# Parts of the projection's matrix on SyncE's queue behind a reading, with rooms of later buffers for odd groups

## The chip, the cores and the metric

The kernel runs on one core of a Trainium2 chip. The metric is device time in microseconds of one execution, as the median of several runs. The engines are TensorE (PE, matmuls; PEld is its weight load), VectorE (DVE), ScalarE (ACT), GpSimd (POOL) and SyncE (SP), which only starts transfers here. A letter q behind an engine's name in the profile (SPq, ACTq) is its instruction queue, with the DMAs that it issues.

## The reference

Two layers over x of 8 sequences x 512 rows x 256 columns, both with a norm before and after and a residual sum: grouped attention, then a mixture of experts. The change touches the last product of the attention (`out @ wo`).

```python
def _L0_attn_ref(x, wq, bq, wkv, bkv, wo):
    G, QPG, D = (4, 4, 128)
    b, t, e = x.shape
    q = (x @ wq + bq).reshape(b, t, G, QPG, D).transpose(0, 2, 3, 1, 4)
    kv = (x @ wkv + bkv).reshape(b, t, G, 1, 2 * D).transpose(0, 2, 3, 1, 4)
    k, v = (kv[..., :D], kv[..., D:])
    pe = sinusoidal_pe(t, D, x.dtype)
    q = q + pe
    k = k + pe
    scores = jnp.einsum('bgqtd,bgksd->bgqts', q, k) / math.sqrt(D)
    scores = jnp.where(causal, scores, -jnp.inf)
    probs = jax.nn.softmax(scores, axis=-1)
    out = jnp.einsum('bgqts,bgksd->btgqd', probs, v).reshape(b, t, G * QPG * D)
    return out @ wo
...
x = x + _layernorm(_L0_attn_ref(_layernorm(x), ...))
x = x + _layernorm(_L0_ffn_ref(_layernorm(x), ...))
```

`_L0_ffn_ref` routes each of the 4096 rows to 6 of 64 experts (at most 64 rows per expert and sequence block) and adds a shared expert. All numbers are float32.

## The kernel before, in words

**Steps.** The attention is a loop over k from 0 to 127: 8 sequences b, in each 4 groups of heads g, in each 4 steps. 16 steps are a sequence; a step handles one quarter of a group's score blocks for 4 heads at once. I number groups through: n = 4 b + g, so group n has the steps 4n to 4n + 3. The order of the instructions on every engine is written out by hand in this loop (`manual_schedule`), and each engine's queue is worked off in that order.

**One step's chain.** `scores(k, q)` (L518 to L526) makes four blocks of scores on TensorE (psc); VectorE adds the mask and takes the smallest (L522), ACT takes the exponential in place (e, L526). `weigh(k)` divides by the sum on GpSimd (L536). In the next step `turned(k)` (L550) turns the weights in 32 x 32 blocks on VectorE into eb (L554), writes eb to DRAM in four DMAs of 160 KB on SyncE's queue (ex_d, L558), waits there for their landing, and reads them back in the other order as et in one DMA of 640 KB (L564). In the step after that `mix(k)` multiplies et with the values on TensorE (pav, L591), and ACT moves the result into ao (L602). So a step's writes and reading stand in step k + 1, and its pav near the end of step k + 2. Two such buffers exist (ex_d[0], ex_d[1]; et with two tiles).

**Other users of SyncE's queue.** Behind the reading come the reading of the next sequence's x, an exchange of normalised rows through DRAM (exr_d; `xr` and `xt`, the latter feeding the shared expert's product psg, L1094), stores of xg, y and the output. ACT's queue carries the store of x1 (L1170), and from step 94 on the experts' weights (wgu, wd: 32 times 352 KB three times over).

**The projection.** For sequences 0 and 7 a step pair's ao is multiplied with a whole group's part of wo (`project`, L616), of which `load_whole` (L204) loads one group at a time (512 KB, tile tag "wc", one buffer). For sequences 1 to 6 (`CROSSED`) it is done by a scheme with seven products instead of eight on sums and differences of blocks: `make_sets` (L625) stores for each of the four groups two sets of blocks in DRAM during sequence 0, ws_d (3 blocks, 384 KB) and wc_d (4 blocks, 512 KB). `straight(j)` (the products ps) uses a ws set, `across(j)` (pc) a wc set, both through `multiply` (L666). `load_set` (L642) loads a group's set, ws into a tile with tag "ws", wc into one with tag "wc", one buffer each. The products of group n stand in steps 4n + 4 to 4n + 7: ps in 4n + 4 and 4n + 6, pc in 4n + 5 and 4n + 7 (for the last group of a sequence both pc stand in even steps or right behind ps).

**When the sets are loaded.** `load_sets(k)` (L1382) is called in step k behind `weigh(k)` and issues on ACT's queue: ws of group n in step 4n + 3, wc of group n in step 4n + 4, that is one step ahead of the products that use them. The whole parts are issued on ACT's queue at the end of steps 6, 10, 14, 114, 118, 122 and 126.

**Semaphores of transfers.** In the built program the DMAs of SyncE and ACT take eight semaphores (DMAHW0 to DMAHW7) in turn. A DMA that takes a semaphore whose last DMA came from the other queue, or is not yet known to have landed, first waits for that landing. So a write of ex_d can wait for a load that ACT issued: in the program before, the fourth write of step 26's weights waits for ws of group 6.

**Buffers that the change borrows.** p3's tag "gx" (three buffers, rows gathered for a pair of experts, L897), p3's "dd" (three buffers, a pair's results, L962) and p2's "gt" (one buffer, L830 and later). The experts' work that uses them begins in step 94.

Of the kernel before, what the change touches and what calls it, by code (L numbers as in the profile page):

```python
# [11 lines left out]
F32 = mybir.dt.float32  # L12
# [7 lines left out]
P = 128  # L20
B, T, E = 8, 512, 256
NT = B * T
NI = T // P
# [4 lines left out]
G, QPG, D = 4, 4, 128  # L28
NH = G * QPG
# [10 lines left out]
EARLY = 5  # L40
# [4 lines left out]
CROSSED = range(1, B - 1)  # L45

@with_exitstack
def sandwich_kernel(ctx, tc, x, wq, bq_t, wkv, bk_t, bv, wo, gate_wt, w_gate, w_up, w_down,
                    sh_gate_t, sh_up_t, sh_down_t, pe_t, out):
    nc = tc.nc  # L50
# [20 lines left out]
    ws_d = [dram.tile([P, 3, 2, P], F32, tag=f"ws{g}_d", name=f"ws{g}_d") for g in range(G)]  # L71
    wc_d = [dram.tile([P, 4, 2, P], F32, tag=f"wc{g}_d", name=f"wc{g}_d") for g in range(G)]
# [83 lines left out]
    with ExitStack() as part:  # L156
        def pool(name, bufs):
            return part.enter_context(tc.tile_pool(name=name, bufs=bufs))

        wpool = pool("weights", 1)  # L160
        p1 = pool("p1", 1)
        p2 = pool("p2", 2)
        p3 = pool("p3", 2)
# [40 lines left out]
        def load_whole(n):  # L204

            t = whole[n] = wpool.tile([D, QPG, E], F32, tag="wc", name=f"wo_{n}")
            nc.scalar.dma_start(out=t, in_=wo.rearrange("(h d) e -> d h e", d=D)[:, ts(n % G, QPG), :])

        load_whole(0)
        partial = wpool.tile([P, 2, 7, P], F32, tag="partial", name="partial")  # L210

        sg_sb, su_sb = [wpool.tile([P, NC, FSH + NX // 2], F32, tag=name, name=name) for name in ("sg_sb", "su_sb")]
        for half, (t, w) in enumerate(((sg_sb, sh_gate_t), (su_sb, sh_up_t))):
            nc.sync.dma_start(out=t[:, :, :FSH], in_=w.rearrange("(c p) n -> p c n", p=P))
            nc.sync.dma_start(out=t[:, :, FSH:],
                              in_=gate_wt.rearrange("(c p) n -> p c n", p=P)[:, :, ts(half, NX // 2)])
# [65 lines left out]
        po = {}  # L282
# [246 lines left out]
        def weigh(k):  # L529
            l = live[k]  # L530
            recip = small.tile([P, NI], F32, tag="recip", name=f"recip_{k}")
            nc.vector.reciprocal(recip, l["total"])  # L532
            engine = nc.gpsimd if k < NK - 1 else nc.vector
            for q in range(NI):
                e = blocks_of(k, q)
                engine.tensor_scalar(e, e, recip[:, q : q + 1], 1.0, ALU.mult, ALU.mult)  # L536
# [82 lines left out]
        crossed, outs, sets = {}, {}, {}  # L619
# [5 lines left out]
        def make_sets(g):  # L625

            w = blocks_of_whole(whole[g])
            t = p1.tile([P, 4, 2, P], F32, tag="xt2", name=f"sets_{g}")
            for k in range(2):
                nc.scalar.dma_start(out=ws_d[g][:, k], in_=w[:, k, 0])  # L630
            nc.scalar.dma_start(out=wc_d[g][:, 0], in_=w[:, 1, 1])
            nc.gpsimd.tensor_sub(t[:, 0], w[:, 0, 1], w[:, 0, 0])
            nc.gpsimd.tensor_sub(t[:, 1], w[:, 1, 1], t[:, 0])
            yield
            nc.gpsimd.tensor_sub(t[:, 2], w[:, 1, 1], w[:, 0, 1])
            nc.gpsimd.tensor_sub(t[:, 3], w[:, 1, 0], t[:, 1])
            yield
            nc.scalar.dma_start(out=wc_d[g][:, 1:], in_=t[:, :3])
            nc.scalar.dma_start(out=ws_d[g][:, 2], in_=t[:, 3])
            yield  # L640

        def load_set(n, d, name):  # L642
            t = wpool.tile(list(d[0].shape), F32, tag=name, name=f"{name}_{n}")
            nc.scalar.dma_start(out=t.rearrange("p k n e -> p (k n e)"), in_=d[n % G].rearrange("p k n e -> p (k n e)"))
            sets.setdefault(n, {})[name] = t

        def sides_of_results(j):

            (x11, x12), (x21, x22) = [[results[j][:, u].rearrange("d (n k) q -> d k n q", k=2)[:, k] for k in range(2)]
                                      for u in range(2)]  # L650
            return x11, x12, x21, x22
# [10 lines left out]
        def multiply(j, factors, name, tag):  # L662
            bank_ = ps_o.tile([P, len(factors[0]), P], F32, tag=tag, name=f"{name}_{j}")
            for pair in range(2):
                for n, (a, w) in enumerate(factors[pair]):
                    nc.tensor.matmul(bank_[:, n, :], lhsT=a, rhs=w, start=pair == 0 and n == 0,  # L666
                                     stop=pair == 1 and n == len(factors[0]) - 1, skip_group_check=True)
            return bank_

        def straight(j):  # L670
            x11, x12, _, x22 = sides_of_results(j)
            w = sets[j // 2]["ws"]
            po[j, 0] = multiply(j, [[(x[:, n], w[:, k, n]) for k, x in enumerate((x11, x12, x22))] for n in range(2)],
                                "ps", "o0")

        def across(j):
            w, t = sets[j // 2]["wc"], crossed.pop(j)
            po[j, 1] = multiply(j, [[(t[:, k, n], w[:, k, n]) for k in range(4)] for n in range(2)], "pc", "o1")

        def add_up(j, part):  # L680
            b, n = divmod(j, 2 * G)
# [26 lines left out]
        def projections(k):  # L708

            j, odd, b, n, last = projected(k)  # L710
            if j < 0:
                return
            if b not in CROSSED:
                for i in () if odd else tiles_at(j):
                    project(j, i)
            elif not odd:
                straight(j)
            elif not last:
                across(j)
# [6 lines left out]
        def projections_behind(k):  # L726
            j, odd, b, n, last = projected(k)
            if b in CROSSED:
                if not odd:
                    add_up(j, 0)  # L730
                elif not last:
                    add_up(j, 1)
                if last and not odd:
                    across(j)
# [644 lines left out]
        values(0, 0, 1)  # L1379
        behind, ahead, making = {}, iter(()), iter(())  # L1380

        def load_sets(k):  # L1382

            n, step = divmod(k, NI)
            if step == 3 and (n // G) in CROSSED:
                load_set(n, ws_d, "ws")
            if step == 0 and n and (n - 1) // G in CROSSED:
                load_set(n - 1, wc_d, "wc")

        routed, zeroing = experts(), zeros()  # L1390
        twice, finishing = False, 0
# [5 lines left out]
        for k in range(NK):  # L1397
# [28 lines left out]
            if k < 2:  # L1426
                queries(k + 2)
            weigh(k)
            load_sets(k)
            if b <= EARLY and s == 7:  # L1430
                next(ahead)()
            side(s, "A")
# [54 lines left out]
            if k % NI == 0 and 1 <= k // NI <= G:  # L1487
                making = make_sets(k // NI - 1)
            next(making, None)
            if k % NI == 2 and k // NI and k // NH not in CROSSED:  # L1490
                load_whole(k // NI)
            side(s, "D")
# [26 lines left out]
        with tc.For_i(0, table["rest"], 1) as n:  # L1519
# [5 lines left out]
            for b in range(EARLY, B):  # L1525
                q, tag = [(p1, "hid"), (wpool, "e0"), (wpool, "e1")][b - EARLY]
                xg = q.tile([P, NI, LROW], F32, tag=tag, name=f"rest_xg_{b}")
                nc.sync.dma_start(out=xg, in_=rows_of(lxg_d, b * T - ET_ROWS))
                q, tag = [(p1, "y"), (p2, "x"), (p1, "xt2")][b - EARLY]
# [73 lines left out]
```

## Time and profile before

| | us |
|---|---|
| three runs | 1398.02, 1405.69, 1407.23 |
| median | 1405.69 |
| profiled execution | 1402.7 |
| its span, first to last instruction | 1400.9 |
| mean granted clock of TensorE | 0.99 |

The profile covers one execution. It lists for each engine the time in which it was busy, for each idle stretch what ended it (the releaser), and for each DMA queue the packets. Queue 1 is SyncE's, queue 10 ACT's:

```profile
## 3 DMA queue, kind: packets, MB, share of 16 engines
q1 hardware_dynamic: 127053, 204.67, 50.2%
q10 hardware_dynamic: 47568, 73.67, 16.3%
q0 software_dynamic: 6144, 9.44, 3.3%
```

The transfers that the following speaks of, with their number and size:

```profile
ex_d<-eb SPq DMA_DIRECT2D x504, 160.0 KB
et<-ex_d SPq DMA_DIRECT2D x126, 640.0 KB
wc<-wc_d ACTq DMA_DIRECT2D x24, 512.0 KB
```

ws is loaded 24 times with 384 KB, whole parts of wo 8 times with 512 KB, all on ACT's queue. In a row of the timeline the first number is the start in us from the span's start, the second the duration, xN the number of instructions merged; the bracket tells how long the engine was idle before it and what ended that. A DMA's row in a queue is its issue, not its transfer.

### The profile page before, as it was taken

The page shows a single profiled execution, that of the slowest core. Times are in us where ns is not written, and L with a number is a line of the kernel's source. Part 1 is how long each engine was busy: PE and PEld are TensorE (multiplying, and loading weights), DVE is VectorE, ACT ScalarE, POOL GpSimd, SP SyncE. Part 2 cuts the span into 40 slices and gives each one's busy share as a digit, 9 for nine tenths or more (in the row PEclk, how much of TensorE's full clock was granted, in tenths as well). Part 3 has the DMA queues.
Part 4 walks back from the last instruction along what each step waited for, and adds up shares of the span by engine and source line. Part 5 has one row for each costly group of instructions (what it writes and reads, how often), then busy time and mean ns, then how long its engine had stood idle before and what let it go on. Part 6 is the DMA issues. An engine that isn't in the chain of part 4 may idle for free. (4 is left out here: it accounts for less than half of the span.)

```text
span 1400.9 us, 22036 instructions
## 1 busy us (share of the span) xinstructions
PE 1333.5 (95%) x6842; PEld 1024.3 (73%) x6842; DVE 917.1 (65%) x2943; ACT 548.4 (39%) x1667; POOL 641.2 (46%) x1052
## 2 busy tenths in 40 slices
PE   9999989999999999999999999998999999989897
PEld 6887776787777776787778776786767677767674
DVE  5575567866777677776787678776557545666544
ACT  3333344334433353334443353333443334434523
POOL 4444243336433553436442553346555554755611
PEclk9999999999999999999999999999999999999999
DMA  6677777655674667655765566679999989877712
GB/s 217 184 235 223 202 222 213 191 163 177 199 206 135 195 189 216 192 160 172 234 184 161 174 206 189 175 214 271 294 312 265 272 237 316 207 240 234 253 59 69
DMA packets 180883, 289.20 MB, mean 206 GB/s; under 512 B 18956, under 2 KB 148461, under 8 KB 180765
## 3 DMA queue, kind: packets, MB, share of 16 engines
q1 hardware_dynamic: 127053, 204.67, 50.2%
q10 hardware_dynamic: 47568, 73.67, 16.3%
q0 software_dynamic: 6144, 9.44, 3.3%
q8 instruction: 55, 0.90, 0.3%
q14 instruction: 63, 0.52, 0.1%
HBM read 172.11 MB, written 115.61 MB: 205 GB/s over the span
## 5 line engine op out<-in xcount | busy, mean ns | idle before, releaser
L536 POOL TENSOR_SCALAR e<-e,recip 128x512 f32<-128x512 f32 (+1 forms) x504 | 245.2, 523 | 507.6 <-DVE recip L532 436.2
L526 ACT ACTIVATE e<-e,least 128x32 f32<-128x32 f32 (+1 forms) x504 | 258.4, 514 | 263.9 <-DVE least L522 243.5
L591 PE MATMUL pav<-et,v 128*128 128x256 f32 x1280 | 307.9, 389 | 41.6 <-DMA et<-ex_d 39.9
L591 PEld LDWEIGHTS pav<-et,v 128*128 128x128 f32 x1280 | 243.6, 194 | 89.9 <-DMA et<-ex_d 23.8
L518 PE MATMUL psc<-kt,qt 128*128 128x32 f32 (+15 forms) x1024 | 276.6, 408 | 3.6 <-DVE least L522 2.2
L522 DVE CUSTOM_DVE_ANT_0 e<-psc,mask 128x32 f32<-128x32 f32 (+1 forms) x504 | 203.9, 430 | 109.0 <-PE psc L518 106.6
L602 ACT ACTIVATE ao<-pav,bv_sb 128x256 f32<-128x256 f32 x255 | 107.2, 471 | 399.8 <-PE pav L591 366.7
L518 PEld LDWEIGHTS psc<-kt,qt 128*128 128x128 f32 x1024 | 161.0, 191 | 64.9 <-DVE least L522 29.1
L554 DVE STREAM_TRANSPOSE eb<-e 128x1024 f32<-128x1024 f32 (+1 forms) x252 | 197.5, 822 | 2.1 <-POOL e L536 1.5
L666 PEld LDWEIGHTS pc<-wc,crossed 128*128 128x128 f32 x768 | 92.5, 192 | 7.8 <-issue 4.3
L666 PE MATMUL pc<-wc,crossed 128*128 128x128 f32 x768 | 94.5, 276 | 0.8 <-POOL crossed L660 0.8
L526 ACT ACTIVATION_READ_ACCUMULATOR e<-e,least 128x1 f32 x504 | 94.4, 187 | 0.0
L666 PEld LDWEIGHTS ps<-ws,ao 128*128 128x128 f32 x576 | 71.6, 192 | 18.2 <-issue 8.4
L971 POOL DMA_INDIRECT y_d<-dd,idx x32 | 50.8, 1588 | 66.7 <-DMA y_d<-dd,idx 22.1
L378 PE MATMUL pq<-xnt,wq_sb 128*128 128x256 f32 x320 | 75.6, 380 | 0.0
L331 DVE SCALAR_TENSOR_TENSOR kt<-pk,bk_sb,pe_sb 128x512 f32<-128x512 f32 x32 | 24.0, 749 | 74.7 <-PE pk L329 72.4
L666 PE MATMUL ps<-ws,ao 128*128 128x128 f32 x576 | 72.3, 275 | 0.3 <-DMA ws<-ws_d 0.3
L422 PE MATMUL pq_back<-rows_joined,heads 128*128 128x256 f32 x264 | 71.3, 379 | 0.0
L340 PEld LDWEIGHTS pv<-wkv_sb,xnt 128*128 128x128 f32 x512 | 65.9, 192 | 4.5 <-issue 1.1
L340 PE MATMUL pv<-wkv_sb,xnt 128*128 128x128 f32 x512 | 67.5, 275 | 0.5 <-ACT ao L602 0.5
L378 PEld LDWEIGHTS pq<-xnt,wq_sb 128*128 128x128 f32 x320 | 59.1, 190 | 10.8 <-issue 1.9
L422 PEld LDWEIGHTS pq_back<-rows_joined,heads 128*128 128x128 f32 x264 | 50.2, 190 | 16.2 <-issue 8.2
(259 smaller groups left out, 1951.9 us busy)
## 6 DMA issues: line engine op xcount, KB each, us to landing
ex_d<-eb SPq DMA_DIRECT2D x504, 160.0 KB
et<-ex_d SPq DMA_DIRECT2D x126, 640.0 KB
wc<-wc_d ACTq DMA_DIRECT2D x24, 512.0 KB
wgu<-in_w_gate ACTq DMA_DIRECT2D x32, 352.0 KB
wgu<-in_w_up ACTq DMA_DIRECT2D x32, 352.0 KB
wd<-in_w_down ACTq DMA_DIRECT2D x32, 352.0 KB
ws<-ws_d ACTq DMA_DIRECT2D x24, 384.0 KB
y<-y_d ACTq DMA_DIRECT2D x10, 512.0 KB
```

Source lines behind the costliest of these rows:

```text
L340: nc.tensor.matmul(pv[:, i, :], lhsT=s["xnt"][:, c, ts(2 * n + i, P)], rhs=wkv_sb[:, c, g, 1, :], start=c == 0, stop=c == NC - 1, skip_gro ...
L378: nc.tensor.matmul(pq[:, n, :, :], lhsT=wq_sb[g][:, c, ts(2 * pair + n, D)], rhs=seqs[b]["xnt"][:, c, :].rearrange("p (u v) -> p u v", v=P ...
L422: nc.tensor.matmul(out, lhsT=factor[0], rhs=factor[1], start=first, stop=last, skip_group_check=True)
L518: nc.tensor.matmul(psc[:, :w], lhsT=halves[k // 2][:, at, :, :].rearrange("d h t -> d (h t)"), rhs=seqs[b]["kt"][g][:, :w], start=True, st ...
L522: nc.vector.tensor_tensor_reduce(out=e, in0=psc[:, :w].rearrange("p (c t) -> p c t", t=BS), in1=mask[:, T - w :].rearrange("p (c t) -> p c ...
L526: nc.scalar.activation(e, e, AF.Exp, bias=l["least"][:, q : q + 1], scale=-1.0, accum_out=l["total"][:, q : q + 1])
L536: engine.tensor_scalar(e, e, recip[:, q : q + 1], 1.0, ALU.mult, ALU.mult)
L554: nc.vector.transpose(eb[:, :, first : first + count, :, :].rearrange("p a j r t -> p j a r t"), weighed[k % 2][:, end - count : end, :, : ...
L591: nc.tensor.matmul(pav[n // NI][:, :, n % 2, :], lhsT=seqs[b]["v"][g][:, j, :], rhs=et[:, :, first + j, :], start=j == 0, stop=j == count ...
L602: nc.scalar.activation(ao, pav[n // NI][:, :, n % 2, :], AF.Identity, bias=bias)
L666: nc.tensor.matmul(bank_[:, n, :], lhsT=a, rhs=w, start=pair == 0 and n == 0, stop=pair == 1 and n == len(factors[0]) - 1, skip_group_chec ...
L971: nc.gpsimd.indirect_dma_start(out=y_d[:, :], out_offset=bass.IndirectOffsetOnAxis(ap=table["idx"][:, m, 1:2], axis=0), in_=pairs.pop(m)[" ...
```

## The change

All loads of sets and of whole parts go from ACT's queue to SyncE's. The sets of odd groups up to 21 are loaded in pieces of one block (128 KB) into other rooms: three ws blocks into the three "gx" buffers, three wc blocks into the three "dd" buffers and the fourth into "gt". Sets of even groups, and of the groups from 23 on, keep the tiles with tags "ws" and "wc". The products take the blocks one by one from a list.

The moments change too: `load_sets` is replaced by a table. For groups 4 to 22 the steps within the sequence are (ws, wc): group 0 at 0 and 2, group 1 at 4 and 5, group 2 at 8 and 11, group 3 at 12 and 13; the sets of group n are then loaded in the steps in which group n - 1's are in use or earlier. From group 23 on they are 4n + 2 and 4n + 3. The call stands near the end of the step, behind `projections_end(k)`, so on SyncE's queue a load issued in step k stands behind the reading of step k - 1's weights and ahead of the writes of step k's.

```diff
         def load_whole(n):
 
             t = whole[n] = wpool.tile([D, QPG, E], F32, tag="wc", name=f"wo_{n}")
-            nc.scalar.dma_start(out=t, in_=wo.rearrange("(h d) e -> d h e", d=D)[:, ts(n % G, QPG), :])
+            nc.sync.dma_start(out=t, in_=wo.rearrange("(h d) e -> d h e", d=D)[:, ts(n % G, QPG), :])
...
-        def load_set(n, d, name):
-            t = wpool.tile(list(d[0].shape), F32, tag=name, name=f"{name}_{n}")
-            nc.scalar.dma_start(out=t.rearrange("p k n e -> p (k n e)"), in_=d[n % G].rearrange("p k n e -> p (k n e)"))
-            sets.setdefault(n, {})[name] = t
+        def load_set(n, which):
+
+            d, count = (ws_d, wc_d)[which][n % G], (3, 4)[which]
+            if n % 2 and n < (EARLY + 1) * G - 1:
+                homes = [((p3, "gx"), (p3, "gx"), (p3, "gx")), ((p3, "dd"), (p3, "dd"), (p3, "dd"), (p2, "gt"))][which]
+                tiles = []
+                for k, (q, tag) in enumerate(homes):
+                    t = q.tile([P, 2, P], F32, tag=tag, name=f"set{which}_{n}_{k}", bufs=3 if q is p3 else 1)
+                    nc.sync.dma_start(out=t.rearrange("p n e -> p (n e)"), in_=d[:, k].rearrange("p n e -> p (n e)"))
+                    tiles.append(t)
+            else:
+                t = wpool.tile([P, count, 2, P], F32, tag=("ws", "wc")[which], name=f"set{which}_{n}")
+                nc.sync.dma_start(out=t.rearrange("p k n e -> p (k n e)"), in_=d.rearrange("p k n e -> p (k n e)"))
+                tiles = [t[:, k] for k in range(count)]
+            sets[n, which] = tiles
...
-            w = sets[j // 2]["ws"]
-            po[j, 0] = multiply(j, [[(x[:, n], w[:, k, n]) for k, x in enumerate((x11, x12, x22))] for n in range(2)],
+            w = sets[j // 2, 0]
+            po[j, 0] = multiply(j, [[(x[:, n], w[k][:, n]) for k, x in enumerate((x11, x12, x22))] for n in range(2)],
                                 "ps", "o0")
...
-            w, t = sets[j // 2]["wc"], crossed.pop(j)
-            po[j, 1] = multiply(j, [[(t[:, k, n], w[:, k, n]) for k in range(4)] for n in range(2)], "pc", "o1")
+            w, t = sets[j // 2, 1], crossed.pop(j)
+            po[j, 1] = multiply(j, [[(t[:, k, n], w[k][:, n]) for k in range(4)] for n in range(2)], "pc", "o1")
...
-        def load_sets(k):
-
-            n, step = divmod(k, NI)
-            if step == 3 and (n // G) in CROSSED:
-                load_set(n, ws_d, "ws")
-            if step == 0 and n and (n - 1) // G in CROSSED:
-                load_set(n - 1, wc_d, "wc")
+        loads = {}
+        for n in range(CROSSED[0] * G, (CROSSED[-1] + 1) * G):
+            if n >= (EARLY + 1) * G - 1:
+                at = (NI * n + 2, NI * n + 3)
+            else:
+                at = [n // G * NH + first for first in ((0, 2), (4, 5), (8, 11), (12, 13))[n % G]]
+            for which, first in enumerate(at):
+                loads.setdefault(first, []).append((n, which))
...
             weigh(k)
-            load_sets(k)
...
             next(making, None)
+            for n, which in loads.get(k, ()):
+                load_set(n, which)
             if k % NI == 2 and k // NI and k // NH not in CROSSED:
                 load_whole(k // NI)
```

## The prediction

> **What bounds the kernel now.** I read the page's busy times first, then the stretches, then TensorE's waits, then the queue of SyncE in the stretch that matters.
>
> ```profile
> PE 1333.5 (95%) x6842; PEld 1024.3 (73%) x6842; DVE 917.1 (65%) x2943; ACT 548.4 (39%) x1667; POOL 641.2 (46%) x1052
> ```
>
> TensorE is idle for only 67 us of 1400.9. No change of queues can be worth more, and what it is worth is read from those waits. By stretch (first column: length; then each engine's busy time, granted clock, DMA share, GB/s):
>
> ```profile
> 0.00:180.00 180.00, 171.66 (x788) 136.83 (x789) 106.71 (x336) 66.74 (x211) 74.52 (x147) 1.00 0.73 215
> 180.00:860.00 680.00, 647.97 (x3302) 509.84 (x3301) 485.20 (x1521) 274.88 (x856) 299.98 (x528) 0.99 0.64 187
> 860.00:1215.00 355.00, 347.69 (x1983) 253.71 (x1982) 217.58 (x716) 135.75 (x397) 189.33 (x255) 1.00 0.88 257
> 1215.00:1401.00 186.00, 166.14 (x774) 123.93 (x772) 107.59 (x372) 70.99 (x204) 77.33 (x123) 0.97 0.56 172
> ```
>
> Half of the idle time, 32 us, lies in 180 to 860, where the matrix's parts are loaded over and over beside little other traffic. TensorE's waits there (total, times, longest):
>
> ```profile
> PE pav L591 <- DMA et<-ex_d: 21.9, 16, 2.1
> PE psg L1094 <- DMA xt<-exr_d: 6.9, 4, 2.1
> PE psc L518 <- DVE least L522: 1.4, 4, 0.3
> ```
>
> So 29 of the 32 us are waits for two transfers that come back through DRAM. SyncE's queue in two steps of that stretch, then TensorE's line there:
>
> ```profile
> 488.23 0.34 SPq L564 DMA_DIRECT2D et<-ex_d  x1
> 493.81 1.89 SPq L558 DMA_DIRECT2D ex_d<-eb  x4
> 499.29 0.34 SPq L564 DMA_DIRECT2D et<-ex_d  x1
> 499.73 2.29 SPq L558 DMA_DIRECT2D ex_d<-eb  x4
> 507.67 0.34 SPq L564 DMA_DIRECT2D et<-ex_d  x1
> ```
>
> ```profile
> 504.33 2.40 PE L591 MATMUL pav<-et,v 128*128 128x256 f32 x10 [1.95 <-DMA et<-ex_d]
> ...
> 512.24 2.43 PE L591 MATMUL pav<-et,v 128*128 128x256 f32 x10 [0.97 <-DMA et<-ex_d]
> ```
>
> I call the four writes and the reading of step k "exchange k" and k mod 16 its place. These are exchanges 50 and 51, places 2 and 3. ACT starts ws at 494.59, inside the writes of 50, and wc at 500.67, inside those of 51. From the last write's issue to the reading it took 3.6 and 5.6 us; where no part is loaded, as at place 1, 2.4. The readings themselves took 4.9 and 4.5 us to land; undisturbed 3.9 (landings here and below are from the trace's DMA records). Of the 16 pav waits, 15 (21.0 us) and all four psg waits are at places 2, 3, 6, 14 and 15, and each of those has a ws or wc load of ACT beside it. The other is at place 13, beside a store of y. SyncE itself is held too:
>
> ```profile
> SPq L564 <- DMA ex_d<-eb: 223.7, 119, 6.2
> SPq L558 <- DVE eb L554: 192.4, 59, 9.6
> SPq L558 <- DMA ws<-ws_d: 39.3, 8, 6.5
> SPq L558 <- DMA wc<-wc_d: 8.8, 4, 4.5
> ```
>
> Twelve times a write of the exchange waits for ACT's load to land, because both take the same one of the eight DMA semaphores in turn. In the built program after the change no write between 180 and 860 waits for a load on ACT's queue but the store of x1.
>
> **The change, term by term.**
>
> Loads leave the old places (2, 3, 6, 7, 10, 11, 14, 15). A ws beside an exchange costs it about 2.2 us (1.2 on the writes, 1.0 on the reading, exchange 50), a wc 3 to 5 us (exchanges 35, 51, 67). Every wait of TensorE in question is 2.1 us or less, so without the loads all can go: 21.0 + 6.9 + 0.3 (one product waiting for ws itself) = **-28.2 us**. Bounds: 0 and -28.2.
>
> Loads arrive in front of exchanges at places 0, 2, 4, 5, 8, 11, 12, 13, behind the reading before. What they push back is the writes. The distance from a reading's landing to the pav that needs it is 4 to 8 us at places 0 (once 1.7), 8, 11 and 12, so nothing shows there. It is 0.1 at place 2, 0.1 to 4.2 at 4, 1.0 at 5 (once 5.7), 0.1 to 0.9 at 13. But at 13 the writes come 6 us after the last landing, at 2 they come 1.7 us after it (once at it), and SyncE sends the load at once: it moves while the queue would be empty. At place 5 the writes start between 2.1 us after and 2.0 us before the landing. What a transfer directly ahead costs is seen at place 0: the writes of exchange 48 start 0.8 us after a 640 KB reading and land 2.9 us after their last issue instead of 2.3. I take 1 us for each of the four place 5 exchanges: **+4 us**. Upper bound, no gap anywhere: a 512 KB part ahead costs 2.1 us (exchange 31, first issue to landing 6.3 against 4.2) and 384 KB 1.6 (three quarters of it, an estimate); less the distances above, over all loads up to exchange 93, at places 2, 4, 5, 8 to 12 and 13: 10 + 2.7 + 4.5 + 0.6 + 7.4 = 25 us. Lower bound 0.
>
> Pieces: 63 transfers of 128 KB for 18 whole ones. Packets of 1 KB took 46 ns in the median, of 3 KB 121, of 4 KB 159: a part then occupies the 16 engines 1.5 us instead of 1.3, 0.2 us where it is hidden. SyncE gets 101 more issues at 0.34 to 0.45 us, up to 1.8 us per part, between a reading and writes for which it waits 192 us on VectorE anyway; the 1 us above holds what is left. If that cover went, the 18 odd-group parts would cost 1 us each more. TensorE executes as many matmuls, and 17 semaphore instructions fewer. ACT loses 56 issues of 0.35 us; TensorE's waits for ACT in the stretch are 0.5 us: nothing.
>
> Given back: with its waits gone TensorE is 99% busy there, and exchanges at places 5, 13, 14, 15 have only 0.0 to 1.2 us to spare, while the writes start when VectorE has turned the weights. I let a quarter of the waits come back as others: **+7 us** (bounds 0 and 14).
>
> A rule that speaks against the first term: the Trainium skill, DMA: Bandwidth & Descriptors, section Issuing engines are not separate DMA queues, says that transfers from different issuing engines run on the same 16 engines and interleave, so that the choice of issuer saves only its own issue time. That ACT's loads slow SyncE's writes agrees with it; by it the queue is worth nothing, and the first term would have to come from the new moments alone.
>
> Other stretches: before 180 three loads of wo (512 KB) move behind readings; TensorE waits 4.3 us there in all, and only one of these waits (0.6 us) has a wo beside it; writes now queue behind it instead: 0, bounds -2 and +2. From 860 to 1215 twelve loads move by one step (the first by three), and five of them now wait on SyncE for a semaphore of an expert load of ACT (longest such wait today 5.3 us). From exchange 99 on readings are 3 to 17 us early; before it one is not: TensorE waits 3.5 us at 978, with ws beside. -1, bounds -5 and +8. After 1215: pav waits of 10.3 us, of which 1.6 have a wo beside: -1, bounds -2 and +2.
>
> Sum: -28.2 + 4 + 7 - 1 - 1 = **-19.2 us**. The profiled execution took 1402.7 us (span 1400.9 and 1.8 around it): 1383.5. The median of the runs, 1405.69, is 3.0 above it, so I predict **1386.5 us**.
>
> **The rivals.**
>
> *The wait changes its name.* TensorE, freed, runs into VectorE's turning and the writes behind it sooner than I allow: half of the 28 us returns. For it: 59 waits of the writes for eb, and places 13 to 15 without slack. Against: psc waits only 1.4 us for VectorE, which is 71% busy in the stretch. -14.1 + 4 - 2 = -12: 1394.
>
> *The wait moves with the load.* The same bytes go through the same engines, and each part delays the exchange that it now precedes by its whole time: -28.2 + 25 - 2 = -5, 1400.5. For it: places 2 and 13 have no slack. Against: the idle queue before the writes at 2 and 13. This is the time that the rule of the Trainium skill above would give.
>
> *Slower: the part ahead is as dear as the part beside.* If at places 2, 4 and 5 a part in front of the writes costs what it costs beside them today (wc 3.1 + 2.0, ws 2.2), then, less the distances to pav, 25 + 5 + 16 = 46 us come, and 30 go: +16, 1421.5. It decides from two thirds of that price. Against: the 0.7 us behind a 640 KB reading at place 0.
>
> That the loads do not stand where the change says is excluded by the built order: each follows a reading, and waits at most for a product on the old part that precedes the pav then running.
>
> **How the numbers follow.** Forecast 0.62, the wait renamed 0.16, the wait moved 0.12, slower 0.10. The range: low is the first term in full with nothing given back, place 5 free at half and the other stretches half way to their best, -28.2 + 2 - 4.5 = -31, 1375; high reaches past the wait moved, 1403. Left out: the slower case and some 0.08 beyond the ends. One per cent, about what a measurement here can tell, is 14 us, so faster means under 1391.6. The forecast reaches that nearly always (0.58), renamed seldom (0.04): faster 0.62, same 0.28, slower 0.10.
>
> **What would show it.** Right: pav's waits for et in the stretch down from 21.9 to under 9 us and psg's from 6.9 to under 3; SyncE's rows of waits for ws and wc gone; readings at places 2, 3, 6, 14 and 15 landing 3.9 to 4.4 us after issue. Moved wait: pav waits at places 2, 5 and 13 instead. Renamed: psc or pq waiting for VectorE. Slower: writes at places 2, 4, 5 landing over 3 us after their last issue. A wait over 5 us of SyncE for an expert load, with a late reading, would break the term of 860 to 1215.

## The result, and the profile after

| | before | after |
|---|---|---|
| runs, us | 1395.84 to 1407.23 (5) | 1378.64 to 1387.72 (5) |
| median, us | 1402.02 | 1381.73 |
| profiled execution, span, us | 1400.9 | 1377.4 |

The ratio is 0.9865, 95% interval 0.9818 to 0.9912. The change made the kernel faster by 1.35%. TensorE did the same matmuls; this is the page's line of the kernel after:

```profile
PE 1324.2 (96%) x6842; PEld 1021.1 (74%) x6842; DVE 915.5 (66%) x2943; ACT 548.3 (40%) x1667; POOL 639.5 (46%) x1052
```

The first two stretches (length, then the engines' busy time, granted clock, DMA share, GB/s):

```profile
0.00:180.00 180.00, 168.09 (x758) 132.95 (x759) 102.53 (x322) 62.58 (x198) 73.51 (x145) 0.99 0.72 208
180.00:860.00 680.00, 662.17 (x3424) 525.27 (x3423) 505.17 (x1589) 284.23 (x884) 306.77 (x544) 1.00 0.67 196
```

In the same 680 us TensorE executes 3424 matmuls instead of 3302. Before 180 it executes 758 instead of 788: that part became slower. TensorE's waits in the middle stretch (total, times, longest):

```profile
PE pav L591 <- DMA et<-ex_d: 7.5, 7, 2.6
PE psc L518 <- DVE qt L457: 2.7, 4, 1.0
PE pav L591 <- ACT e L526: 1.8, 1, 1.8
PE pav L591 <- DVE shift_o L104: 1.5, 3, 0.6
```

By these rows the wait for et fell from 21.9 to 7.5, and psg's (6.9) is gone. The pav rows that name ACT or VectorE are no new waits: e, shift_o or xg are nothing that pav reads. The profile names the update that came last, and in each of these waits the reading's last packet had landed 0.4 to 0.6 us before, as in the waits that name et. Here it is exchange 52, whose last packet landed 0.5 us ahead of pav:

```profile
509.88 0.34 SPq L564 DMA_DIRECT2D et<-ex_d  x1
514.22 1.97 PE L591 MATMUL pav<-et,v 128*128 128x256 f32 x8 [1.45 <-DVE xg L117]
```

Counted by the readings' landings, between the products of steps 17 and 85 (from about 180 to 840 us), pav's waits for et fell from 22.5 to 11.2 us: 7.0 of them at place 4, 3.1 at place 2 and 1.1 at place 5. What is new is that psc waits for VectorE's qt (2.7 us, 0.2 before). SyncE's queue around exchanges 50 and 51, then TensorE's line:

```profile
481.89 0.34 SPq L564 DMA_DIRECT2D et<-ex_d  x1
482.27 0.43 SPq L654 DMA_DIRECT2D set<-wc_d  x1
487.47 1.87 SPq L558 DMA_DIRECT2D ex_d<-eb  x4
491.84 0.34 SPq L564 DMA_DIRECT2D et<-ex_d  x1
493.14 2.37 SPq L558 DMA_DIRECT2D ex_d<-eb  x4
498.12 0.34 SPq L564 DMA_DIRECT2D et<-ex_d  x1
```

```profile
496.45 2.40 PE L591 MATMUL pav<-et,v 128*128 128x256 f32 x10 [0.42 <-DVE shift_o L104]
...
503.23 2.32 PE L591 MATMUL pav<-et,v 128*128 128x256 f32 x10
```

The set wc is issued behind the reading of exchange 49, and 5.2 us pass before the next write. From the last write's issue to the reading it is now 2.5 and 2.6 us; before it was 3.6 and 5.6. SyncE's own waits show something new:

```profile
SPq L558 <- DVE eb L554: 196.3, 59, 7.7
SPq L564 <- DMA ex_d<-eb: 175.3, 138, 4.0
SPq L558 <- DMA x_d<-x: 23.5, 5, 5.2
```

The rows for ws and wc are gone, and the wait for the writes' landing fell from 223.7 to 175.3 us. But a write of exchange 20, 36, 52, 68 and 84 (place 4) now waits for ACT's store of x1 to land, through a shared semaphore.

To see where the time came from I mark the kernel by two matmuls, the first of pav 17 and the first of pav 85, and read their start from TensorE's timeline. Idle is TensorE's time without a matmul. A slow stretch is a run of matmuls that together took over 1 us longer than the median distance of the same shapes.

| us | to pav 17 (idle) | pav 17 to 85 (idle) | rest (idle) | slow stretches, middle |
|---|---|---|---|---|
| before | 178.3 (8.3) | 665.6 (31.5) | 548.6 (19.3) | 4, 7.1 us |
| after | 186.1 (13.7) | 639.8 (15.3) | 543.4 (16.1) | none |

So in these two executions the middle gave 25.8 us, the end 5.2, and the beginning lost 7.8. The runs of one kernel spread by about 10 us, so the smaller two need other runs beside them, and get them below. Of the 25.8, 16.2 are idle time and 7.1 are slow stretches that had followed long waits; 2.5 are spread thinly.

### The profile page after: what moved, and what is told of

Same layout as the page of the kernel before. It is cut to its first block, busy times and chain, and to the rows that moved or that the text cites. A ratio compares the mean times of both kernels' runs of the same rounds, so it can differ in the third digit from the quotient of the medians.

```text
span 1377.4 us, 22075 instructions
## 1 busy us (share of the span) xinstructions
PE 1324.2 (96%) x6842; PEld 1021.1 (74%) x6842; DVE 915.5 (66%) x2943; ACT 548.3 (40%) x1667; POOL 639.5 (46%) x1052
## 5 line engine op out<-in xcount | busy, mean ns | idle before, releaser
L591 PE MATMUL pav<-et,v 128*128 128x256 f32 x1280 | 302.3, 383 | 33.7 <-DMA et<-ex_d 26.5
L591 PEld LDWEIGHTS pav<-et,v 128*128 128x128 f32 x1280 | 240.5, 191 | 79.0 <-issue 13.4
L677 PEld LDWEIGHTS pc<-set,crossed 128*128 128x128 f32 x768 | 92.5, 192 | 7.8 <-issue 4.3
L677 PE MATMUL pc<-set,crossed 128*128 128x128 f32 x768 | 94.5, 276 | 0.8 <-POOL crossed L671 0.8
L677 PEld LDWEIGHTS ps<-set,ao 128*128 128x128 f32 x576 | 71.7, 192 | 17.6 <-issue 9.1
L677 PE MATMUL ps<-set,ao 128*128 128x128 f32 x576 | 72.2, 275 | 0.0
L422 PEld LDWEIGHTS pq_back<-rows_joined,heads 128*128 128x128 f32 x264 | 50.2, 190 | 16.2 <-issue 8.2
```

The lines of the kernel that those rows point to most:

```text
L422: nc.tensor.matmul(out, lhsT=factor[0], rhs=factor[1], start=first, stop=last, skip_group_check=True)
L591: nc.tensor.matmul(pav[n // NI][:, :, n % 2, :], lhsT=seqs[b]["v"][g][:, j, :], rhs=et[:, :, first + j, :], start=j == 0, stop=j == count ...
```

## The experiments

My theory when I began was that sharing between two queues is the harm: a load on ACT's queue takes engines from an exchange, one on SyncE's own queue stands behind the reading and leaves it alone. The rivals: only the moment counts, or only the shared semaphores. Two marks show queue and moment below: Q for the sets on SyncE, M for the changed moments.

**The queue alone** (Q, not M).

```diff
 def load_set(n, d, name):
...
-    nc.scalar.dma_start(out=t.rearrange("p k n e -> p (k n e)"), in_=d[n % G].rearrange("p k n e -> p (k n e)"))
+    nc.sync.dma_start(out=t.rearrange("p k n e -> p (k n e)"), in_=d[n % G].rearrange("p k n e -> p (k n e)"))
```

> The kernel before with one word changed: ws and wc are issued on SyncE's queue instead of ACT's, in the same steps and into the same tiles; wo stays on ACT. Sharing between queues (my theory): a load on the exchange's own queue starts behind the reading and leaves it alone, so pav's waits for et in the stretch fall from 21.9 to under 10 us and readings land 3.9 to 4.5 us after issue; 17 to 24 us less than before (about 0.985). The moment decides (rival): same steps, same bytes, so the waits stay, 1.00. Shared semaphores (rival): the twelve waits of SyncE for ws and wc are gone, so as the first theory, 0.985.

Measured: 1.0419 (1.0384 to 1.0453), slower by 4%. No theory had that. TensorE's first and fourth wait in 180 to 860 of this run:

```profile
PE ps L666 <- DMA ws<-ws_d: 56.9, 12, 7.4
...
PE pav L591 <- DMA et<-ex_d: 0.7, 1, 0.7
```

SyncE and TensorE in one such step:

```profile
348.00 0.34 SPq L564 DMA_DIRECT2D et<-ex_d  x1
348.38 0.43 SPq L644 DMA_DIRECT2D ws<-ws_d  x1
```

```profile
353.38 2.71 PE L666 MATMUL ps<-ws,ao 128*128 128x128 f32 x12 [4.18 <-DMA ws<-ws_d]
```

The load stands behind a reading that SyncE starts only when the writes have landed. It goes out at 348.4 and lands at 353.2, and ps of the next step has been waiting for it for 4.2 us. pav's waits vanish (in part because TensorE, held up at ps, also comes to pav later), but ws itself is late. For ws, one step ahead of its product is not early enough behind a reading; wc, moved in the same way, kept no pc waiting in this stretch.

**The moments alone** (M, not Q): in the kernel after, all three `nc.sync` of `load_set` and `load_whole` become `nc.scalar`, as here for the pieces.

```diff
 def load_set(n, which):
...
-    nc.sync.dma_start(out=t.rearrange("p n e -> p (n e)"), in_=d[:, k].rearrange("p n e -> p (n e)"))
+    nc.scalar.dma_start(out=t.rearrange("p n e -> p (n e)"), in_=d[:, k].rearrange("p n e -> p (n e)"))
```

> The kernel after with all sets and wo issued on ACT's queue again, at the changed moments and into the changed rooms. Sharing between queues: loads run beside readings and writes again, now of other places, so most of the gain is gone, 0.995 to 1.01. The moment decides: the gain stays, 0.985. Shared semaphores: the built order has 37 writes or parts of exchanges that take turns with a piece on ACT and 19 with a whole set, five times as many as before, so slower than before, 1.00 to 1.02, with SyncE's waits for sets over 48 us.

Measured: 0.979 (0.9761 to 0.9819). The whole gain is there without the queue, and my theory fell. The semaphores' forecast fell too: 56 parts take turns with the exchanges here, and SyncE waited 13.5 us for sets between 180 and 860, against 48 before. pav waited 8.1 us for et in the middle, counted by landings, and the middle took 635.1 us.

**A third queue** (the kernel before, `nc.scalar` to `nc.gpsimd` in `load_set`).

> The kernel before with ws and wc issued on GpSimd's queue, whose transfers take no turn with SyncE's eight semaphores; steps and tiles as before. Shared semaphores: SyncE's waits for ws and wc (48 us) are gone and pav's waits go with them, 0.985. Sharing between queues: the loads still run beside the exchanges from another queue, pav's waits stay over 15 us in the stretch, 0.995 to 1.005. The first or the second of these also says whether the writes or the readings are what is late: with sharing the readings take 4.5 us and more.

Measured: 1.0095 (1.0058 to 1.0131). pav's waits for et fell to 0.2 us, but pc waited 22.4 us for wc and ps 9.6 for ws: GpSimd issued the loads later (wc of one group at 351.4 where ACT had it at 343.5). As with SyncE, a load that is issued later spares the exchange and keeps the product waiting. It doesn't tell the semaphores from the sharing.

**The rooms alone, twice.** First the changed rooms and pieces with everything on ACT and `at = (NI * n + 3, NI * n + 4)`, the old steps:

> The changed rooms and pieces, all sets and wo on ACT's queue, but issued in the steps of the kernel before (ws of group n in step 4n + 3, wc in 4n + 4). If it is the moments that brought the gain, the waits for et are back at places 2, 3, 6, 14 and 15 (over 15 us in the stretch), 0.995 to 1.005. If the rooms and the pieces brought it (a piece holds an engine for less long, and a load need not wait for the room), 0.98 to 0.985. If shared semaphores count, slower than before: 69 parts take turns with writes of exchanges, 1.00 to 1.02.

Measured: 1.0233 (1.0183 to 1.0284). This miss was mine: the loop over `loads` stands at the end of a step, where the kernel before had its call behind `weigh(k)`. So the loads were later than before, and the costliest wait in the middle says so:

```profile
PE pc L677 <- DMA set<-wc_d: 19.7, 16, 4.5
```

Then with the call moved back to its old place:

```diff
 weigh(k)
+for n, which in loads.get(k, ()):
+    load_set(n, which)
...
-for n, which in loads.get(k, ()):
-    load_set(n, which)
```

> The changed rooms and pieces, all sets and wo on ACT, and the loads called where the kernel before calls them: in steps 4n + 3 (ws) and 4n + 4 (wc) right behind the weights' division. In the run before this one they stood at the end of these steps, came some 10 us later than in the kernel before (wc at 354 instead of 343 us), and TensorE waited 29 us for the sets themselves, so that run said nothing of rooms. Moments decide: pav's waits for et are back, over 15 us in the stretch, 0.995 to 1.005. Rooms and pieces decide: 0.98 to 0.985. Pieces are dear on ACT: over 1.005.

Measured: 0.9986 (0.9958 to 1.0013), and the old waits are back (the two costliest in 180 to 860):

```profile
PE pav L591 <- DMA et<-ex_d: 21.8, 14, 3.2
PE psg L1105 <- DMA xt<-exr_d: 7.4, 4, 2.0
```

Rooms and pieces are worth nothing that shows by themselves. Loads later than at the old place cost 2.5% (1.0233 / 0.9986), and at the old place they meet the exchanges without slack. The gain is in the earlier moments, which the borrowed rooms make possible.

**The queue's worth once the moments are changed.** The kernel after carries two side effects: the loss before 180 and the wait for x1. I took each away, then both.

```diff
 def load_whole(n):
...
-    nc.sync.dma_start(out=t, in_=wo.rearrange("(h d) e -> d h e", d=D)[:, ts(n % G, QPG), :])
+    nc.scalar.dma_start(out=t, in_=wo.rearrange("(h d) e -> d h e", d=D)[:, ts(n % G, QPG), :])
```

> The kernel after with only wo's loads on ACT's queue again. From the start of the first pav to that of step 17 the kernel after took 7.8 us more than before, 5.2 of it at steps 9 and 10, where the reading of step 9 had wo right behind it and landed after 8.3 us instead of 4.7. If wo on SyncE is the cause, those 5 to 8 us go: 0.981 to 0.983 of before, the start of pav 17 near 178.5. If it is the drift of the zero stores and of ACT's set stores in that stretch (rival), pav 17 still starts after 184 and the ratio stays 0.9865.

Measured: 0.9859 (0.9821 to 0.9898). pav 17 starts at 180.9 instead of 186.1, and the reading of exchange 9 took 5.4 us instead of 8.3. This pair alone would put 5.2 of the 7.8 us down to wo. But two runs below (x1 on GpSimd, and the turns moved) have the same instructions as the kernel after up to there, and pav 17 starts at 182.9 in both, with readings of 6.9 and 6.6 us; with the moments changed and wo on ACT's queue, five runs have it at 179.5 to 180.9. So wo on SyncE cost between 2.0 and 6.6 us. The rest of the kernel took 547.3 instead of 543.4, and the times alone don't separate this run from the kernel after. What wo did there is plain in the kernel after, SyncE first, then TensorE:

```profile
102.35 0.34 SPq L564 DMA_DIRECT2D et<-ex_d  x1
102.78 0.39 SPq L207 DMA_DIRECT2D wo<-in_wo  x1
```

```profile
110.79 3.81 PE L591 MATMUL pav<-et,v 128*128 128x256 f32 x10 [3.90 <-DMA et<-ex_d]
```

With wo 0.4 us behind it, the reading was unfinished until 110.7. wc right behind the reading of exchange 49 had not done that (4.0 us).

```diff
 def store():
-    (nc.scalar if b < EARLY else nc.sync).dma_start(out=rows_of(x1_d, b * T), in_=xt)
+    (nc.gpsimd if b < EARLY else nc.sync).dma_start(out=rows_of(x1_d, b * T), in_=xt)
```

> The kernel after with the store of x1 on GpSimd's queue for sequences 0 to 4. In the kernel after a write of exchange 20, 36, 52, 68 and 84 (place 4) waits for the landing of that store, 23.5 us of SyncE in all, and pav then waits 2.65, 0.49, 1.45, 1.12 and 1.28 us, 7.0 together. If the shared semaphore is the cause, these waits go and the time is 4 to 7 us less than the kernel after, 0.981 to 0.984 of before. If the store's transfer beside the writes is the cause (rival), the writes at place 4 still land late, pav still waits over 4 us there, 0.985 to 0.988.

Measured: 0.9811 (0.9769 to 0.9853). The middle took 627.7 us instead of 639.8, with 5.2 idle instead of 15.3; SyncE's wait for x1 is gone, and with it pav's 7.0 us of waits at place 4. But GpSimd started the store 4 us behind the first write (348.9 and 344.8), where ACT had started it 1 us behind (353.3 and 352.2). So the semaphore and the transfer beside the writes were both taken away. To part them I moved only the turns of the semaphores in the kernel after:

```diff
 def store():
+    for i in range(4 if b < EARLY else 0):
+        tiny = p1.tile([1, 8], F32, tag="tiny", name=f"tiny_{b}_{i}", bufs=6)
+        nc.scalar.dma_start(out=tiny, in_=wq[0:1, :8])
     (nc.scalar if b < EARLY else nc.sync).dma_start(out=rows_of(x1_d, b * T), in_=xt)
```

> The kernel after with four loads of 32 bytes on ACT's queue ahead of each store of x1, which move the turns of the eight semaphores: of the writes at place 4 only one of exchange 20 still waits for the store, those of 36, 52, 68 and 84 don't, while the store stays on ACT's queue (at most 1.6 us later). Semaphore: pav's waits at place 4 of 0.49, 1.45, 1.12 and 1.28 us go, 3 to 5 us less than after, 0.982 to 0.985. Transfer: the writes beside the store land as late as in the kernel after, the waits stay, 0.986 to 0.988.

Measured: 0.9876 (0.9841 to 0.9911). Inconclusive: SyncE now waited 19.2 us for the small loads, ahead of the third piece of ws:

```profile
345.22 0.34 SPq L564 DMA_DIRECT2D et<-ex_d  x1
345.60 5.00 SPq L650 DMA_DIRECT2D set<-ws_d  x3
350.71 3.30 SPq L558 DMA_DIRECT2D ex_d<-eb  x4
```

The last write went out 8.8 us behind the reading's issue, as in the kernel after, and pav waited 6.3 us at place 4. The wait had changed its object, not its length, and how much of x1's cost is semaphore and how much transfer stays open.

With both edits the sets alone are left on SyncE (Q and M):

> The kernel after with wo on ACT's queue and the store of x1 on GpSimd's: only the sets are still on SyncE's queue. If the queue of the sets is worth nothing either way once the moments are changed, this equals the run with everything on ACT, 0.976 to 0.981. If sets directly ahead of the writes on SyncE's queue cost something by themselves, it stays at 0.983 or above, with pav's waits at places 2, 4 and 5.

Measured: 0.9766 (0.9719 to 0.9814). And with the sets on ACT as well (M, not Q), x1 on GpSimd:

> All sets and wo on ACT at the changed moments, and the store of x1 on GpSimd's queue. In the run with the store on ACT, SyncE waited 2.2 us for it and the exchanges at place 4 had 0.1 to 0.2 us to spare or less, with readings of 4.6 to 5.5 us that ran beside pieces of wc. If the store matters there, 2 to 4 us less than that run, 0.976 to 0.978; if not, the same, 0.979.

Measured: 0.9775 (0.9733 to 0.9816). The two are the same within the measurement, 630.0 and 633.7 us in the middle: with the moments changed and the side effects gone, the queue of the sets has no worth that shows in the time. The traces do differ a little: in the middle pav waited 3.0 us for et with the sets on SyncE (2.0 in the run with x1 alone on GpSimd) and 6.7 with them on ACT's queue. Some 4 us, 0.3%, are less than these runs can tell. Both are the fastest versions of the study, about one per cent below the kernel after (0.9766 / 0.9865 = 0.990). TensorE is busy for 97% of the span of the first:

```profile
PE 1321.8 (97%) x6842; PEld 1020.7 (75%) x6842; DVE 918.1 (67%) x2943; ACT 547.6 (40%) x1667; POOL 643.9 (47%) x1057
```

**Which moments.** The same kernel (sets on SyncE, wo on ACT, x1 on GpSimd) with the sets of sequences 1 to 5 one step later:

```diff
-((0, 2), (4, 5), (8, 11), (12, 13))
+((1, 3), (5, 6), (9, 12), (13, 14))
```

> The run with sets on SyncE, wo on ACT and x1 on GpSimd (0.9766 of before), with every set of sequences 1 to 5 one step later: places 1, 3; 5, 6; 9, 12; 13, 14. Every set still comes a step or more ahead of its product. If it is only the earliness that counts, 0.975 to 0.98. If it counts which exchange's writes stand behind the load, the exchanges at places 3, 6 and 14 (0 to 3 us to spare) are late now: 6 to 15 us of pav's waits for et come back in the stretch, 0.982 to 0.99.

Measured: 0.9807 (0.9771 to 0.9842), which overlaps with 0.9766. The traces part them: the middle took 643.9 us instead of 630.0, and pav waited 13.2 us for et, counted by landings, instead of 3.0; 8.1 of them at place 3, where it waited in each of the five sequences. One of them, SyncE, then TensorE:

```profile
489.35 0.34 SPq L564 DMA_DIRECT2D et<-ex_d  x1
489.73 0.43 SPq L654 DMA_DIRECT2D set<-wc_d  x1
490.74 2.69 SPq L558 DMA_DIRECT2D ex_d<-eb  x4
497.70 0.34 SPq L564 DMA_DIRECT2D et<-ex_d  x1
```

```profile
503.45 1.83 PE L591 MATMUL pav<-et,v 128*128 128x256 f32 x6 [2.51 <-DMA et<-ex_d]
```

The writes follow the load by 1.0 us here and not by 5.2 as at place 2. Then the queue doesn't help: from the last write's issue to the reading it is 4.3 us. The empty time ahead of the writes decides, for either queue: in the run with the moments alone, ACT issued the same set 3.5 us ahead of the writes of exchange 50, and there it was 2.5 us.

**The slow stretches.** In the kernel before:

```diff
 def mix(k):
...
+    if b in CROSSED and k % NH in (2, 3, 6, 14, 15):
+        for i in range(8):
+            nc.tensor.matmul(pav[0][:, 0, :, :].rearrange("p u t -> p (u t)"), lhsT=ident, rhs=wq_sb[0][:, 0, :2 * HALF],
+                             start=True, stop=True, skip_group_check=True)
```

> The kernel before with eight matmuls of 128 x 128 (an estimate of 1.0 us together, from ps, whose twelve take 1.5 us) into pav's bank ahead of pav in the steps of places 2, 3, 6, 14 and 15 of sequences 1 to 5, whose results pav overwrites. They do nothing but work where TensorE waits for et. In the kernel before four of those waits (1.9 to 2.1 us) were followed by some 4 us at a granted clock of 0.5 to 0.65, in which the work took 1.7 to 1.8 us longer. If it is the idleness that draws the clock down, these slow stretches are gone or fewer (0 to 1 in 180 to 860), pav's waits shrink by the matmuls' time, and the total is 0 to 7 us less than before (0.995 to 1.00; 1 us is lost in each step that did not wait). If the clock falls for another reason, three to five slow stretches stay and the total is 1.00 to 1.005.

Measured: 1.0128 (1.0088 to 1.0168). My estimate of the matmuls was half of the truth: the eight took 1.95 us, as 16 records, since a float32 matmul shows as two. All 30 groups (the edit reaches sequence 6 too) took 58.5 us. The span grew by only 11.3 us (1412.2), mainly because idle time fell by 33.5 us in all and the slow stretches of the middle from four (7.1 us) to one (1.8 us). That one follows the longest wait for et that the extra work left:

```profile
199.60 3.90 PE L595 MATMUL pav<-et,v 128*128 128x256 f32 x10 [2.04 <-DMA et<-ex_d]
```

So the slow stretches come from the idleness (the last section shows how), and a wait can cost nearly twice its length.

## Why the prediction was right, and where not

The forecast was a sum of -19.2 us; the median fell by 20.3 and the profiled span by 23.5. Term by term:

*The waits of 180 to 860.* -28.2 with +4 for place 5 and +7 given back made -17.2. Idle time in the middle fell by 16.2. That the two are close is luck, for the parts are not. The first term was too large: counted by landings, pav still waits 11.2 us for et, so 18.4 of 29.6 went. 7.0 of what stayed is at place 4 (2.65, 0.49, 1.45, 1.12 and 1.28 us). The prediction named the store of x1 there as the one wait that remains, and gave it no price; that is the missing term. Against that, place 5 cost 1.1 instead of 4, and the other waits grew by 2.2, not by 7.

*What the sum left out.* It counted waits at their length. The four slow stretches behind them, 7.1 us, went too. They stood in the profile of before: pav at 355.85 took 3.59 us behind its wait, at 504.33 only 2.40.

*Before 180.* "0, bounds -2 and +2" failed: +7.8 here, +4.6 in the two other runs with wo on SyncE. The row that it used, one wait of 0.6 us beside a wo, said what wo costs in ACT's queue, not what it costs 0.4 us behind a reading. This error and the 7.1 us left out nearly cancel, and the sum is closer to the result than its parts are.

*After 860.* -2; the part behind pav 85 gave 5.2 in the two profiles. Two other runs with the same instructions there (x1 on GpSimd, and the turns moved) took 545.0 and 549.5 us instead of 543.4, against 548.6 before, so that not even the sign is shown. No experiment went into it.

*The cause.* The prediction gave the gain to loads that stop meeting exchanges, and left open whether queue or moment does it. The moment does it, shown by 0.979 with the sets on ACT and by 0.9766 against 0.9775. SyncE's waits for ws and wc fell with the moment (48 to 13.5 us) though more parts take turns. How much of the old harm was semaphore can be bounded from the trace of before: the twelve waits of SyncE for ws and wc stand in exchanges at places 6, 7 and 10. pav waited 2.0 us at place 6 and not at the other two, and psg's 6.9 us come from a transfer that stands in the queue behind the writes of place 6. The remaining 20.5 of 29.4 us are at places where no write waited for a load's semaphore.

*The rule.* The Trainium skill, DMA: Bandwidth & Descriptors, section Issuing engines are not separate DMA queues, has transfers of different issuers interleave on the same engines. The runs agree with it (0.9766 and 0.9775). The step that failed was mine: I let the rule stand for the rival at 1400.5. It says that the queue is worth nothing, and the sentence behind it had already said what follows, that the gain would have to come from the moments.

*The rivals and marks.* The mark for pav, under 9 us, is met by the profile's rows (7.5) and missed by the landings (11.2); the marks for psg and for SyncE's rows are met. Renaming happened to a small part: psc's waits for VectorE's qt rose from 0.2 to 2.7 us. At place 5, which had no wait before, pav waited 1.1 us; at place 2 it waited 3.1 where it had waited 9.7. Writes at place 5 landed 2.6 to 3.2 us after their last issue, at 2 and 4 under 2.5: the mark of the slower case (over 3) was passed by a little at one place of three. Readings at places 3, 14 and 15 landed 3.7 to 4.1 us after issue, as said; beyond the mark's 4.4, at place 2 they took up to 5.0, and at place 6 of the first four sequences 4.6 to 6.0, beside the reading of the normalised rows.

## What to carry to other kernels

Before a load is moved to another queue, move it in time on the queue where it is: here the moment gave 2.1% and the queue nothing that shows in the time, and the queue alone lost 4% because a load behind a reading goes out later. The place to look for is the empty time between a reading and the next writes (5.2 us at one place, 1.0 at the next), and a borrowed room is worth what it lets a load come earlier. When a transfer changes its queue or moment, ask which other transfer now waits with it: at the store of x1, untouched by the change, TensorE waited 7.0 us afterwards, at place 5 only 1.1. And where the profile names an engine whose result the waiting one doesn't read, look for a transfer that landed just then.

## What the runs showed of the hardware

TensorE's clock falls behind some waits, and the traces show which. In each trace the granted clock is at half for 3.41 us at a time, or twice that (longer or odd lengths only at the end of the span), and these stretches lie on one grid: in the kernel before, the four of the middle start at 189.71, 356.96, 541.28 and 814.35, which is 49, 54 and 80 times 3.413 us apart. What counts is how much of a wait falls into one window of this grid. Here are two windows and what follows each, first the wait of 1.88 us at 355.85, then the one of 1.95 us at 504.33:

```profile
353.55:356.96 3.41, 1.53 (x7) 1.02 (x7) 2.45 (x12) 0.61 (x2) 2.48 (x5) 1.00 0.99 276
356.96:360.37 3.41, 3.41 (x10) 2.70 (x9) 0.00 (x0) 0.84 (x2) 0.70 (x2) 0.50 0.29 81
500.32:503.73 3.41, 2.06 (x11) 1.50 (x10) 2.38 (x9) 2.09 (x6) 2.25 (x5) 1.00 0.98 265
503.73:507.14 3.41, 2.81 (x15) 2.58 (x16) 0.18 (x1) 1.87 (x5) 3.41 (x7) 1.00 0.72 268
```

The first wait lies in one window, which is idle for 1.88 us, and the clock is halved in the next. The second is cut by the grid into 1.36 and 0.60 us, and nothing follows. In the kernel after, the waits of 2.65 us (at 215) and 3.58 us (at 1216) are cut likewise, into 1.29 and 1.36 and into 1.86 and 1.72, and drew nothing; of the one of 3.90 us, 2.59 fell into one window, and it did. Over the fourteen traces, from 35 to 1290 us, 60 of 62 slow stretches follow a window that was idle for 1.86 us or more, and every window at the full clock that was idle for 2 us or more was followed by one; between 1.86 and 1.98 both happen. The other two, after 1.27 and 1.61 us, are unexplained. Each of the four of the middle cost 1.74 to 1.79 us, about half of 3.41.

The Trainium skill, TensorE: Matmul & The Clock Gate, section Part 1: The HAM clock gate, describes a free-running window of some 3.4 us whose idleness halves the clock. The traces agree with the window, but it need not be idle throughout: some 1.9 us of it were enough here.

Loads of 512 KB behind a reading of 640 KB on the same queue behaved differently. wc left the reading at 4.0 us. With wo 0.4 us behind the reading of exchange 9 and beside two stores of ACT, the reading took 8.3, 6.9 and 6.6 us in three runs, and 4.2 to 5.7 in the eleven with wo on ACT's queue. But in the kernel after another part of wo, 1.3 us behind the reading of exchange 5 and also beside two such stores, left that reading at 3.9 us. So wo and the stores together don't suffice; whether it is the 0.4 us wasn't tried.
